# Attention values by stationary weights, carried by DMA and turned on VectorE, in a shifted-window transformer block on one core

## The chip, the cores and the metric

One Trainium2 chip, one core of it. The metric is the device time in microseconds (us) of one execution. The kernel before has a median of 2818.03 us over three runs (2814.11 to 2820.3).

## What is computed

The input x is 16 images of 192 channels, 56 x 56 pixels, float32. Layer 0 is a Swin block with 7 x 7 windows shifted by 3, six heads of 32 channels; layer 1 is a masked 3 x 3 depthwise convolution whose taps depend on the image's mean. Cut to what matters:

```python
win = shifted_windows(layernorm(x))            # (windows, 49 positions, 192 channels)
q, k, v = split(win @ qkv_w + qkv_b)           # six heads of 32 channels
attn = softmax(q @ k.T * 32**-0.5 + bias + mask)   # 49 x 49 for each window and head
out = (attn @ v) @ proj_w + proj_b             # back to the image, added to x
x1 = x + out
y = x1 + gelu(layernorm(x1) @ fc1_w + fc1_b) @ fc2_w + fc2_b
out = depthwise_conv3x3(y, taps(mean(y)))      # four of nine taps are not masked
```

The change concerns v, and how `attn @ v` reads it.

## The kernel before, in words

An image is cut into four units (`NU = 4`), each of 2 x 8 windows: channels lie in three groups (`G = 3`) of 64 partitions, and the two halves of the 128 partitions hold two rows of windows, called `ab`. So there are 64 units, and a tile such as `xs1` is 128 x 3 x 392 values, 392 being eight windows of 49 positions. All arithmetic is float32.

The kernel is one software pipeline: a Python loop over r, one round for each unit and a few rounds before and after. In a steady round r the code lists, in this order: both halves of the values of unit r with the scores of unit r between them; the scaling of the next units' inputs on POOL (`scaled2`, `scaled1`); `weighted(r-1)`, that is attention times values; the second MLP layer of unit r-3; the projection of unit r-1; queries and keys of unit r+1; the first MLP layer of unit r-2; the products of the variances (`deviations`); convolution pieces of an image that is complete; and the load of a later unit. In the rounds with r below 3, queries and keys come directly after values and scaling.

Nothing is issued in that listing. Each step is registered with `add(engine, duration, function, reads, writes)`. `Plan.order` then fixes one order for every engine: TensorE's steps stay in the order listed, and the other engines take, by assumed durations and due times, whichever ready step is most urgent. On the chip, each engine runs its fixed order and waits where an input is not there. SyncE issues nearly all DMAs in such an order too.

TensorE writes to four PSUM tiles (`ps0` to `ps3`, two banks each). `bank()` hands them out in rotation, so every product waits until the reader of the product four places earlier has emptied its tile.

Names and lines that matter:

- `values` (L656) multiplies with the windows stationary: for each window the 64 columns of `xs1` from its first position are loaded as weights, 15 of them not the window's own, and `wqkv` (192 columns) moves through. Positions therefore come out on partitions, as `weighted` needs them. `keep` (L668, ScalarE) copies each half into `v`, of which there are two buffers.
- `scores` (L551) multiplies queries (`q128`, `q2`) by keys (`kbd`, `kbd2`) in three groups; then VectorE adds the bias (L577), takes maxima (L587) and sums (L604), POOL subtracts and scales (L592, L610), and ScalarE takes the exponential (L599).
- `turn_shares` (L621) transposes the shares in 32 x 32 blocks on VectorE into `tt`, and ten DMAs (L627) carry them to `pt`, keys on partitions.
- `weighted` (L692) multiplies `v`, stationary, by `pt`; ScalarE (L719) and VectorE (L721) copy the result.
- `second_layer` (L839) ends in L826 on VectorE, `projection` (L762, L748) in L790, `first_layer` (L801) in the GELU of L813 on ScalarE. `queries_keys` is L471; VectorE writes `kbd` from it in L495.
- `deviations` (L320): ScalarE squares (L334), VectorE subtracts (L341), ScalarE takes logarithm and exponential (L350, L357), a DMA goes out (L367) and two come back (L376) into `rb`, which `scaled1` (L427, L438) and `scaled2` (L456) read. L385 is its form for the first units.
- `conv` runs on VectorE in L1114; `taps` has its product at L921.

Of the kernel before, what the change touches and what calls it, by code (L numbers as in the profile page):

```python
# [14 lines left out]
G = 3  # L15
# [3 lines left out]
NWIN = IMG // WS  # L19
N = WS * WS  # L20
UT = NWIN * N
UP = UT + 16
PW = 64 + N
NU = 4
LR = NU * WS
# [20 lines left out]
class Plan:  # L46
# [7 lines left out]
    def add(self, eng, dur, fn, reads=(), writes=(), lag=0.0, slack=60.0, by=None):  # L54
        i = len(self.ops)
        deps = set()
        reads, writes = flat(reads), flat(writes)
        for k in reads:
            if k in self.writer:
                deps.add(self.writer[k])  # L60
        for k in writes:
            if k in self.writer:
                deps.add(self.writer[k])
            deps.update(self.readers.get(k, ()))
        for k in reads:
            self.readers.setdefault(k, []).append(i)
        for k in writes:
            self.writer[k] = i
            self.readers[k] = []
        deps.discard(i)  # L70
        self.ops.append((eng, dur, fn, sorted(deps), lag, slack, by))
# [70 lines left out]
def tile_swin_then_dynamic_conv(  # L142
# [37 lines left out]
    def sb(name, *shape):  # L180
        return const.tile(list(shape), F32, tag=name, name=name)
# [20 lines left out]
    hid = sb("hid", 128, NFC, 2, UT)  # L202
    fold = sb("fold", 128, 2, 2, UT)
    sq = sb("sq", 128, G, UT)
    xs1 = sb("xs1", 128, G, UP)
    xs2 = sb("xs2", 128, G, UT)
    rb = sb("rb", 128, 2, UT)
    q128 = sb("q128", 128, 2, NWIN, 2, TL)
# [3 lines left out]
    e_t = [sb(f"e{i}", 128, 16 * N + TL) for i in range(3)]  # L212
    tt = sb("tt", 128, 2, 48, TL)
    pt = sb("pt", 128, 2, 48, TL)
    v = [sb(f"v{i}", 128, 2, 4, DIM) for i in range(2)]
    o1 = sb("o1", 128, 2, NWIN, N)
    o2 = sb("o2", 128, 2, NWIN // 2, N)
    bt1 = sb("bt1", 128, 2, 2, 4, 2, N)
# [40 lines left out]
    def P(j):  # L259
        return slice(64 * j, 64 * j + 64)  # L260
# [185 lines left out]
    def XS1(s):  # L446
        return [("xs1", g) for g in range(G)] + [
            ("xs1", "w", 0),
            ("xs1", "w", WS - SHIFT),
        ]  # L450
# [163 lines left out]
    def turn_shares():  # L614
        for j in range(3):
            for kb in range(2):
                def turn(kb=kb, j=j):

                    src = e_t[j][:, kb * TL : kb * TL + 16 * N]
                    src = src.rearrange("p (k t) -> p k t", t=N)[:, :, 0:TL]  # L620
                    nc.vector.transpose(tt[:, kb, 16 * j : 16 * j + 16], src)  # L621
                add("DVE", 0.7, turn, [("e", j), "epad"], [("t", j, kb)])
        def send(name, kb, to, of, qb):
            add(
                "SP",
                0.65,
                lambda: nc.sync.dma_start(pt[to, qb], tt[of, kb]),  # L627
                [("t", j, kb) for j in range(3)] + ["ptz"],
                [("pt", name, kb, qb)],
                lag=7.0,  # L630
            )


        for kb, n in ((0, TL), (1, 16)):
            for w in range(2):
                for qb in range(2):
                    to, of = 64 * w + TL * kb, 64 * w + TL * qb
                    send(w, kb, slice(to, to + n), slice(of, of + n), qb)
        for qb in range(2):
            send(2, 1, slice(N - 1, 128, 64), slice(TL * qb + 16, 128, 64), qb)  # L640

    def PTK():
        return [("pt", i, kb, qb) for kb in range(2) for i in range(2 + kb) for qb in range(2)]

    def values(s, parts):
        d = xs1
        for t in parts:
            p, pk = bank()

            def product(t=t, p=p):  # L650
                for i in range(2):
                    w0 = 4 * t + 2 * i
                    for g in range(G):
                        for w in (w0, w0 + 1):
                            for ab in range(2):
                                nc.tensor.matmul(  # L656
                                    p[P(w % 2), ab, i * DIM : (i + 1) * DIM],
                                    d[P(ab), g, w * N : w * N + 64],
                                    wqkv[P(ab), g, 2 * DIM :],
                                    start=(g == 0),  # L660
                                    stop=(g == G - 1),
                                    tile_position=(64 * ab, 64 * (w % 2)),
                                )

            add("PE", 1.95, product, XS1(s) + ["wqkv", "xpad"], [pk])

            def keep(t=t, p=p):
                nc.scalar.copy(  # L668
                    v[s % 2][:, :, 2 * t : 2 * t + 2, :].rearrange("p a w c -> p a (w c)"),
                    p[:, :, 0 : 2 * DIM],  # L670
                )

            add("ACT", 0.87, keep, [pk], [("v", s % 2, t)])

    def weighted(s):


        banks = [bank() for _ in range(3)]

        def product(j):  # L680
            p = banks[j][0]
            for t in range(4):
                for h in range(2):
                    for w in range(2):
                        if j < 2:
                            ab, pair, lane = j, t, 64 * h
                            slot, head = 16 * j + h * 8 + pair * 2, 2 * h
                        else:
                            ab, pair, lane = t // 2, 2 * h + t % 2, 64 * h
                            slot, head = 32 + ab * 8 + pair * 2, 4  # L690
                        shares = pt[P(w), :, slot : slot + 2, 0:QL]
                        nc.tensor.matmul(  # L692
                            p[lane : lane + 64, w, t * 128 : t * 128 + 4 * QL],
                            v[s % 2][P(w), ab, pair, head * HD : (head + 2) * HD],
                            shares.rearrange("p q k c -> p k q c"),
                            start=True,
                            stop=True,
                            tile_position=(64 * w, lane),
                        )

        for j in range(3):
            p, k = banks[j]
            add(
                "PE",
                0.7,
                lambda j=j: product(j),
                PTK() + [("v", s % 2, t) for t in range(2)] + ["ptz"],
                [k],
            )
            for i in range(4):  # L710
                lanes = slice(TL * i, TL * i + TL)
                at = (i % 2) * 2 * QL
                src = p[lanes].rearrange("p w (t c) -> p w t c", c=128)[:, :, :, at : at + N]
                if j < 2:
                    dst = o1[lanes, j].rearrange("p (t w) c -> p w t c", w=2)
                else:
                    dst = o2[lanes].rearrange("p a (t w) c -> p w (a t) c", w=2)
                if j != 1:
                    add("ACT", 0.5, lambda dst=dst, src=src: nc.scalar.copy(dst, src), [k], [("o", j, i)])  # L719
                else:  # L720
                    add("DVE", 0.56, lambda dst=dst, src=src: nc.vector.tensor_copy(dst, src), [k], [("o", j, i)])  # L721
# [466 lines left out]
    def masks():  # L1188
        def go():
            nc.vector.memset(mask2, 0.0)  # L1190
            for i in range(4):
                nc.vector.memset(mask2[i * TL : (i + 1) * TL, i % 2 : i % 2 + 1], 1.0)
        add("DVE", 0.5, go, [], ["mask2"])
        def go():
            nc.gpsimd.memset(q128, 0.0)
            nc.gpsimd.memset(q2, 0.0)
        add("POOL", 1.5, go, [], ["qpad"])
        def go():
            nc.gpsimd.memset(xs1[:, :, UT:UP], 0.0)
        add("POOL", 0.3, go, [], ["xpad"])  # L1200
        def go():
            for t in e_t:
                nc.gpsimd.memset(t[:, 16 * N :], 0.0)
        add("POOL", 0.3, go, [], ["epad"])
        def go():
            nc.gpsimd.memset(pt, 0.0)
        add("POOL", 3.0, go, [], ["ptz"])
        add("POOL", 0.2, lambda: nc.gpsimd.memset(zero, 0.0), [], ["zero"])
# [334 lines left out]
    for r in range(-2, S + 3):  # L1543
# [22 lines left out]
        early = r < 3  # L1566
        norms = [n for n, s in ((0, r + 2), (1, r - 1)) if has(s) and not early]
        if has(r):
            values(r, (0,))
            scores(r)  # L1570
            values(r, (1,))
        if 2 <= r <= 3:
            deviations([1])
        if has(r - 2):
# [12 lines left out]
            fold_proj()  # L1587
        if has(r):
            turn_shares()
        if r == S + 2:  # L1590
            ahead = early_mean(B - 1)
            next(ahead)
            second_layer(S - 1, (0,))
            for _ in ahead:
                pass
            second_layer(S - 1, (1,), lambda: taps(B - 1))
            halos(B - 1, slice(0, 2))
            second_layer(S - 1, (2,))
            halos(B - 1, slice(2, 3))
        elif has(r - 3):  # L1600
            second_layer(r - 3)
# [116 lines left out]
```

## Time and profile before

| quantity | value |
|---|---|
| median of three runs | 2818.03 us |
| the profiled execution | 2820.74 us, span 2818.9 us |
| TensorE busy | 2769.0 us (98% of the span) |
| VectorE busy | 1839.4 us (65%) |
| ScalarE busy | 1674.8 us (59%) |
| GpSimd (POOL) busy | 1582.4 us (56%) |
| moved by DMA | 189.35 MB, mean 67 GB/s |
| mean granted clock of TensorE | 0.993 |

The span runs from the first to the last instruction. Busy times are sums over the whole execution. Lines are given as L656, which is line 656 of the kernel. A steady round takes a little over 42 us. The chain of waits follows the work that ended last back through what released it; its shares are shares of the span.

### The profile page before, as it was taken

How to read it: one execution, taken by the hardware profiler on the slowest of the kernel's cores; microseconds unless marked ns; L12 is line 12 of the kernel's file. 1: busy time of each engine (PE TensorE's matmuls, PEld its weight loads, DVE VectorE, ACT ScalarE, POOL GpSimd, SP SyncE). 2: the span in 40 equal slices, each digit the busy share in tenths (PEclk: the TensorE clock that was granted, in tenths of full speed). 3: DMA queues.
4: the chain of work that ended last, by engine and by line, in shares of the span. 5: the costliest groups of instructions: out<-in, count | busy, mean ns of one | idle time of the engine just before them, and what ended most of it. 6: DMA issues, size and time to landing. Idle time of an engine off the chain costs nothing.

```text
span 2818.9 us, 79781 instructions
## 1 busy us (share of the span) xinstructions
PE 2769.0 (98%) x34405; PEld 1729.2 (61%) x34405; DVE 1839.4 (65%) x3324; ACT 1674.8 (59%) x2532; POOL 1582.4 (56%) x1436
## 2 busy tenths in 40 slices
PE   7899999999999999999999999999999999999998
PEld 5566666666566566566566666566666666665654
DVE  5555776657676675766757666675766757667673
ACT  3656556556566565666656566575565665566553
POOL 5554564565555565664655655655655655646532
PEclk9899999999999999999999999999999999999999
DMA  6412232233313233142233313233142232322131
GB/s 128 82 28 48 59 88 55 63 67 79 78 43 91 44 74 83 44 99 57 51 81 74 84 44 77 54 79 79 43 105 49 56 85 58 83 60 54 42 72 42
DMA packets 122264, 189.35 MB, mean 67 GB/s; under 512 B 31240, under 2 KB 96696, under 8 KB 121912
## 3 DMA queue, kind: packets, MB, share of 16 engines
q1 hardware_dynamic: 117144, 183.43, 29.3%
q8 instruction: 270, 4.42, 0.7%
q10 hardware_dynamic: 4768, 0.82, 0.2%
q14 instruction: 82, 0.67, 0.1%
HBM read 66.81 MB, written 38.98 MB: 38 GB/s over the span
## 4 chain that ended last, share of the span: by engine, by line
PE 95%; DVE 2%; issue 1%; ACT 1%; SPq 0%; DMA 0%; POOL 0%; ACTq 0%; DVEq 0%; POOLq 0%
PE ps L839 27%; PE ps L801 27%; PE ps L471 13%; PE ps L656 9%; PE ps L692 5%; PE ps L762 5%; PE ps L551 5%; PE ps L748 2%; PE ps L320 2%; DVE trow L934 0%; DVE hid L1114 0%; POOL xs L427 0%; DVE x L790 0%; DVE sq L935 0%; PE ps L921 0%
## 5 line engine op out<-in xcount | busy, mean ns | idle before, releaser
L839 PE MATMUL ps<-hid,wf 128*64 128x392 f32 x4608 | 774.1, 494 | 2.5 <-ACT o L719 2.5
L801 PE MATMUL ps<-xs,wf 64*128 64x392 f32 x4608 | 769.5, 489 | 0.0
L801 PEld LDWEIGHTS ps<-xs,wf 64*128 64x128 f32 x4608 | 445.9, 187 | 312.6 <-issue 0.9
L839 PEld LDWEIGHTS ps<-hid,wf 128*64 128x64 f32 x4608 | 330.3, 137 | 409.7 <-issue 370.2
L304 POOL TENSOR_TENSOR fold<-sq 128x392 f32<-128x392 f32 x128 | 131.8, 1029 | 700.5 <-PE ps L320 693.9
L813 ACT ACTIVATE hid<-ps,b1f 128x784 f32<-128x784 f32 x384 | 343.2, 914 | 145.4 <-PE ps L801 142.9
L592 POOL TENSOR_TENSOR e<-e,top 128x784 f32<-128x784 f32 x192 | 285.9, 1504 | 242.0 <-DVE top L587 242.0
L471 PE MATMUL ps<-xs,wqkv 64*128 64x392 f32 x2304 | 406.6, 502 | 11.3 <-POOL xs L438 9.7
L1114 DVE SCALAR_TENSOR_TENSOR y<-x,wt,y 128x770 f32<-128x770 f32 x270 | 305.2, 1145 | 86.1 <-ACT y L977 63.5
L471 PEld LDWEIGHTS ps<-xs,wqkv 64*128 64x128 f32 x2304 | 219.5, 189 | 177.3 <-issue 20.7
L610 POOL TENSOR_TENSOR e<-e,tot 128x784 f32<-128x784 f32 x192 | 293.2, 1537 | 55.4 <-DVE tot L605 53.3
L656 PE MATMUL ps<-wqkv,xs 64*64 64x192 f32 x6144 | 279.6, 325 | 2.1 <-issue 1.8
L456 POOL TENSOR_TENSOR xs<-x,rb 128x392 f32<-128x392 f32 x192 | 247.6, 1318 | 25.3 <-DMA rb<-rsd 25.3
L577 DVE TENSOR_TENSOR e<-ps,bt 128x784 f32<-128x784 f32 x192 | 175.2, 968 | 130.2 <-PE ps L551 130.2
L719 ACT COPY o<-ps 32x392 f32<-32x392 f32 x512 | 246.9, 482 | 9.7 <-PE ps L692 3.5
L621 DVE STREAM_TRANSPOSE tt<-e 128x512 f32<-128x512 f32 x384 | 246.3, 686 | 5.8 <-POOL e L610 4.3
L656 PEld LDWEIGHTS ps<-wqkv,xs 64*64 64x64 f32 x6144 | 225.2, 133 | 37.6 <-issue 24.5
L484 ACT ACTIVATE q<-ps,qbs 128x400 f32<-128x400 f32 (+1 forms) x128 | 68.6, 589 | 287.3 <-PE ps L471 287.3
L604 DVE TENSOR_REDUCE tot<-e 128x16 f32<-128x784 f32 x192 | 182.1, 949 | 64.8 <-ACT e L599 64.7
L341 DVE TENSOR_TENSOR m<-ps,m 128x196 f32<-128x196 f32 (+1 forms) x64 | 23.2, 362 | 304.4 <-ACT m L334 304.3
L668 ACT COPY v<-ps 128x768 f32<-128x768 f32 x128 | 102.4, 800 | 198.2 <-PE ps L656 198.2
L730 ACT ACTIVATE x<-x,pbt 128x392 f32<-128x392 f32 x192 | 105.5, 613 | 189.7 <-POOL xs L438 189.7
(126 smaller groups left out, 3594.0 us busy)
## 6 DMA issues: line engine op xcount, KB each, us to landing
pt<-tt SPq DMA_DIRECT2D x256, 192.0 KB
x<-in_x_dram SPq DMA_DIRECT2D x112, 294.0 KB
out_dram<-y SPq DMA_DIRECT2D x135, 196.0 KB
pt<-tt SPq DMA_DIRECT2D x256, 96.0 KB
rb<-rsd SPq DMA_DIRECT2D x118, 196.0 KB
out_dram<-y SPq DMA_DIRECT2D x45, 154.0 KB
x<-in_x_dram SPq DMA_DIRECT2D x16, 168.0 KB
pt<-tt SPq DMA_DIRECT2D x128, 12.0 KB
```

The lines of the kernel that those rows point to most:

```text
L456: nc.gpsimd.tensor_tensor(xs2[:, g], xv[:, g], rb[:, 1], ALU.mult)
L471: nc.tensor.matmul(p[:, ab, 0:UT], lhs_qk(ab, g, i), d[P(ab), g, 0:UT], start=(g == 0), stop=(g == G - 1), tile_position=(64 * ab, 0),)
L592: nc.gpsimd.tensor_tensor(ev, ev, top[j].broadcast_to([128, 16, N]), ALU.subtract)
L604: nc.vector.tensor_reduce(tot[j], ev, AX.X, ALU.add)
L610: nc.gpsimd.tensor_tensor(ev, ev, tot[j].broadcast_to([128, 16, N]), ALU.mult)
L621: nc.vector.transpose(tt[:, kb, 16 * j : 16 * j + 16], src)
L656: nc.tensor.matmul(p[P(w % 2), ab, i * DIM : (i + 1) * DIM], d[P(ab), g, w * N : w * N + 64], wqkv[P(ab), g, 2 * DIM :], start=(g == 0), s ...
L719: add("ACT", 0.5, lambda dst=dst, src=src: nc.scalar.copy(dst, src), [k], [("o", j, i)])
L801: nc.tensor.matmul(p[:, ab, 0:UT], wf1[P(ab), g, f * 128 : (f + 1) * 128], xs2[P(ab), g], start=(g == 0), stop=(g == G - 1), tile_position ...
L813: nc.scalar.activation(hid[:, f], p[:, :, 0:UT], AF.Gelu, bias=b1f[:, f : f + 1])
L839: nc.tensor.matmul(p[P(ab), 0, 0:UT], wf2[:, f, g * 64 : (g + 1) * 64], hid[:, f, ab], start=(f == 0), stop=(f == NFC - 1), tile_position= ...
L1114: nc.vector.scalar_tensor_tensor(dst, s_, w[:, g, t : t + 1], dst, ALU.mult, ALU.add)
```

## The change

`values` is one function of three products instead of two halves. The weights are now stationary, 64 output channels at a time, and the windows move through them: four windows of 49 positions in one matmul. Channels therefore come out on partitions, and the result must be turned. ScalarE copies it out of PSUM in two pieces per product, the first 32 positions of each window and the last 17. Their destination, `cut`, is the memory of `kbd`, which the scores have read by then. Eight DMAs on SyncE's queue move it to the new tile `vb`, blocks of 32 keys to the partitions where they belong. `turn_values` transposes `vb` in 32 x 32 blocks on VectorE into `v`, which now has one buffer. All three products come after the scores, and the turn is listed after `turn_shares`. `weighted` reads 49 partitions instead of 64, so the padding of `xs1` and its memset go.

```diff
-    def values(s, parts):
...
-                                nc.tensor.matmul(
-                                    p[P(w % 2), ab, i * DIM : (i + 1) * DIM],
-                                    d[P(ab), g, w * N : w * N + 64],
-                                    wqkv[P(ab), g, 2 * DIM :],
...
+    def values(s):
+        cut = kbd.rearrange("p a w h t -> p (a w h t)")[:, 0 : 2 * 8 * G * TL]
+        cut = cut.rearrange("p (b w g t) -> p b w g t", b=2, g=G, t=TL)
+        ck = [("kbd", 0), ("kbd", 1)]
+        xw = xs1.rearrange("p g (w i t) -> p g w i t", i=2, t=N)
+        for m in range(G):
+            p, pk = bank()
+            def product(m=m, p=p):
+                for g in range(G):
+                    for wh in range(2):
+                        for ab in range(2):
+                            nc.tensor.matmul(
+                                p[P(wh), ab, 0 : 4 * N],
+                                wqkv[P(ab), g, 2 * DIM + 64 * m : 2 * DIM + 64 * m + 64],
+                                xw[P(ab), g, :, wh],
+                                start=(g == 0),
+                                stop=(g == G - 1),
+                                tile_position=(64 * ab, 64 * wh),
+                            )
+            add("PE", 0.99, product, XS1(s) + ["wqkv"], [pk])
+            for b, n in ((0, TL), (1, N - TL)):
+                def keep(m=m, p=p, b=b, n=n):
+                    src = p[:, :, 0 : 4 * N].rearrange("p a (w t) -> p a w t", t=N)
+                    dst = cut[:, b, :, m, 0:n].rearrange("p (a w) t -> p a w t", a=2)
+                    nc.scalar.copy(dst, src[:, :, :, TL * b : TL * b + n])
+                add("ACT", 0.45 if b == 0 else 0.36, keep, [pk], ck if m == 0 and b == 0 else [("cut", m, b)])
+        done = [("cut", m, b) for m in range(G) for b in range(2)] + ck
+        for wh in range(2):
+            for i in range(2):
+                for b in range(2):
+                    def go(wh=wh, i=i, b=b):
+                        of, to = 64 * wh + TL * i, 64 * wh + TL * b
+                        nc.sync.dma_start(
+                            vb[to : to + TL, i].rearrange(flat_),
+                            cut[of : of + TL, b].rearrange(flat_),
+                        )
+                    add("SP", 0.65, go, done, [("vb", wh, i, b)], lag=4.0)
+    def turn_values():
+        for i in range(2):
+            def turn(i=i):
+                dst = v.rearrange("p a w (g i c) -> p (a w g) i c", g=G, i=2)[:, :, i]
+                nc.vector.transpose(dst, vb[:, i].rearrange("p w g t -> p (w g) t"))
+            add("DVE", 1.05, turn, [("vb", wh, i, b) for wh in range(2) for b in range(2)], [("v", i)])
...
         if has(r):
-            values(r, (0,))
             scores(r)
-            values(r, (1,))
+            values(r)
...
             turn_shares()
+            turn_values()
```

More of the change, by code (lines that the diff above doesn't have):

```diff
@@ L21 @@
 UT = NWIN * N
-UP = UT + 16
 PW = 64 + N
@@ L204, in tile_swin_then_dynamic_conv @@
     sq = sb("sq", 128, G, UT)
-    xs1 = sb("xs1", 128, G, UP)
+    xs1 = sb("xs1", 128, G, UT)
     xs2 = sb("xs2", 128, G, UT)
@@ L214, in tile_swin_then_dynamic_conv @@
     pt = sb("pt", 128, 2, 48, TL)
-    v = [sb(f"v{i}", 128, 2, 4, DIM) for i in range(2)]
+    v = sb("v", 128, 2, 4, DIM)
+    vb = sb("vb", 128, 2, 8, G, TL)
     o1 = sb("o1", 128, 2, NWIN, N)
@@ L643, in PTK @@
         return [("pt", i, kb, qb) for kb in range(2) for i in range(2 + kb) for qb in range(2)]
-    def values(s, parts):
-        d = xs1
-        for t in parts:
-            p, pk = bank()
[L650 to L656, printed above, removed]
-                                    p[P(w % 2), ab, i * DIM : (i + 1) * DIM],
-                                    d[P(ab), g, w * N : w * N + 64],
-                                    wqkv[P(ab), g, 2 * DIM :],
[L660 to L673, printed above, removed]
@@ new lines, in values @@
+    def values(s):
[4 more added lines that the diff above has]
+        for m in range(G):
+            p, pk = bank()
+            def product(m=m, p=p):
[18 more added lines that the diff above has]
+        done = [("cut", m, b) for m in range(G) for b in range(2)] + ck
+        flat_ = "p w g t -> p (w g t)"
+        for wh in range(2):
[8 more added lines that the diff above has]
+                    add("SP", 0.65, go, done, [("vb", wh, i, b)], lag=4.0)
@@ L690, in product @@
                             slot, head = 32 + ab * 8 + pair * 2, 4
-                        shares = pt[P(w), :, slot : slot + 2, 0:QL]
+                        shares = pt[64 * w : 64 * w + N, :, slot : slot + 2, 0:QL]
                         nc.tensor.matmul(
                             p[lane : lane + 64, w, t * 128 : t * 128 + 4 * QL],
-                            v[s % 2][P(w), ab, pair, head * HD : (head + 2) * HD],
+                            v[64 * w : 64 * w + N, ab, pair, head * HD : (head + 2) * HD],
                             shares.rearrange("p q k c -> p k q c"),
@@ L706, in weighted @@
                 lambda j=j: product(j),
-                PTK() + [("v", s % 2, t) for t in range(2)] + ["ptz"],
+                PTK() + [("v", i) for i in range(2)] + ["ptz"],
                 [k],
@@ L1198, in go @@
         def go():
-            nc.gpsimd.memset(xs1[:, :, UT:UP], 0.0)
-        add("POOL", 0.3, go, [], ["xpad"])
-        def go():
             for t in e_t:
```

## The prediction

> **What bounds the kernel now.** I read the page first: busy times, then the chain that ended last.
>
> ```profile
> PE 2769.0 (98%) x34405; PEld 1729.2 (61%) x34405; DVE 1839.4 (65%) x3324; ACT 1674.8 (59%) x2532; POOL 1582.4 (56%) x1436
> ...
> PE 95%; DVE 2%; issue 1%; ACT 1%; SPq 0%; DMA 0%; POOL 0%; ACTq 0%; DVEq 0%; POOLq 0%
> ```
>
> TensorE is 98% busy and 95% of the chain, with values (L656) at 9% of the span. Every other engine idles a third of the time or more, so TensorE time removed is worth its full length until another engine arrives too late. The chain through one steady round says where it stands:
>
> ```profile
> 1160.63 0.80 PE ps L320 x16
> 1161.43 2.11 PE ps L656 x48
> 1163.54 2.08 PE ps L551 x96
> 1165.62 1.95 PE ps L656 x48
> 1167.57 2.26 PE ps L692 x96
> 1169.83 12.00 PE ps L839 x72
> 1181.83 1.99 PE ps L762 x24
> 1183.82 1.16 PE ps L748 x24
> 1184.98 6.12 PE ps L471 x36
> 1191.10 11.85 PE ps L801 x72
> ```
>
> Each line begins where the one before ends: no wait at all. I call the end of L320, 1161.43, time zero of a round. What must be on time for it are the shares, the scaled inputs and emptied PSUM tiles. The timelines of SyncE and VectorE, and the stretch of DMA in which the shares travel, give the slack:
>
> ```profile
> 1161.89 0.36 DVE L341 TENSOR_TENSOR m<-ps,m 128x196 f32<-128x196 f32 x1 [0.84 <-ACT m L334]
> 1164.28 2.74 DVE L577 TENSOR_TENSOR e<-ps,bt 128x784 f32<-128x784 f32 x3 [2.03 <-PE ps L551]
> ...
> 1194.81 6.61 SPq L627 DMA_DIRECT2D pt<-tt  x10
> ...
> 1197.00:1201.50 4.50, 4.50 (x32) 2.60 (x30) 1.20 (x2) 3.86 (x6) 0.00 (x0) 1.00 1.05 213
> ```
>
> VectorE was idle before L341 (0.84 us) and before the biases (2.03 us). The ten share DMAs were all issued at 1201.4 and read by L692 from 1209.7: 8.3 us of slack, landing included. The last line's final columns are DMA share and GB/s: the engines kept up with the issue, at 213 GB/s.
>
> **What the Trainium skill says.** "TensorEngine Tiling (Array Packing)", section 64×64 Mode, gives four tiles that work side by side; both forms use all four. The trace agrees: L551's 96 instructions of 98 columns take 2.02 to 2.08 us, 0.86 ns per column over four tiles. Its section PSUM Bottleneck warns that emptying PSUM may become the limit; here the four-tile rotation decides, worked out below. "DMA: Bandwidth & Descriptors", section Anatomy of one DMA, gives about 2 us of fixed cost; I use it as an estimate for landing. It was measured on another issuing path, and no row here shows a landing. "VectorE: DVE Perf Modes", section The three transpose paths, says that VectorE turns 32 x 32 blocks only; that is why eight DMAs are needed.
>
> **The change, part by part.**
>
> 1. *Products.* Before: 96 instructions a unit (each matmul is recorded as two) of 192 columns, 2.11 + 1.95 = 4.06 us on the chain. The first half's extra 0.16 is a change of tile shape after L320; L748 shows the same, with 1.16 us for 24 instructions of 196 columns where 24 x 196 / 4 x 0.84 ns (L801: 11.85 us over 72 x 392 / 2 columns) is 0.99. After: 72 instructions of 196 columns, three times L748's 24 without its entry cost: 2.97 us. The entry cost stays, now paid by the scores. So 3.90 - 2.97 = 0.93 us a unit, times 64 = **59.5 us off the chain**. The moving operand is read in runs of 49 instead of 192; L692 reads in runs of 25 and takes 2.06 us in undelayed rounds against 2.02 by columns, so I cost runs at nothing. Bounds: gain of 0.85 to 1.10 us a unit.
>
> 2. *A new PSUM neighbour.* In the order of the changed program the scores come first after L320, and the first values product takes the tile that L320 filled. L341 on VectorE empties it, and the order puts L341 behind the first bias. That bias starts 0.74 us after the scores (1164.28 - 1163.54), takes 0.91, then L341 0.36: it ends at +2.05 to +2.1, against 2.02 to 2.08 for the scores. A wait of 0 to 0.1 us; I take 0.05 in 60 rounds, **3 us back**. Behind this wait stands everything on TensorE. Later tiles are free in time: biases end near +4 (second and third values product need the first two, from +3.1), and `weighted` starts at +5.
>
> 3. *ScalarE.* Two copies of 0.80 us (L668) become six, of 256 and 136 values per partition. From 0.80 us for 768 and 0.48 for 392 (L719): about 0.15 + 0.85 ns each, so 0.37 and 0.27, 1.9 us a unit, 0.3 more. They end near +6; the second copy ended at +7 before, so the copies and exponentials behind them are not later. Hidden.
>
> 4. *Eight DMAs.* SyncE issues one in about 0.65 us (6.61 / 10): 5.2 us, with the two of L376 in the middle of them, so from about +6 to +12.5. That makes the scaled inputs' `rb` later by up to 2 us. POOL began scaling at 1176.07 (+14.6) and finished 5.3 us before L471; with `rb` issued near +10 it still begins on time. 98 KB each is 0.79 MB, under 4 us at 213 GB/s, shorter than their issue; landing by about +14.5. Stores and loads that follow on the queue are not waited for. Hidden; bounds 0 and the second rival.
>
> 5. *VectorE.* Two turns of 768 values: 0.67 us for 512 (L621) gives 1.0 each, 2 us a unit, 129 us in all on an engine with 35% idle. The order puts them after the first two share turns, around +17, and before L826 of the third second-layer product (ends at 2.05 + 2.97 + 2.2 + 12.0 = +19.2). Queued behind is L826, with the projection's adds and, each fourth round, the mean and `taps`, whose product is due at +21.2. Turns ending at +19.3 leave all on time. The last share turns wait for POOL and L471, not for this. `weighted` comes 1.1 us earlier in the round, so its 8.3 us of slack becomes 6 to 7. Hidden.
>
> 6. *`kbd` as carrier.* Steady rounds overwrite it at +26, long after landing. In rounds 0 to 2 L471 follows directly. In round 1 the changed order puts `kbd`'s copies behind a sum and three share turns, and the second `weighted` product uses their tile: I estimate 5 us there from the durations of those rows, and 2 us more because these rounds wait for POOL anyway and cannot pocket their gain. **7 us back**, bounds 2 and 15. The dropped memset was hidden by the start.
>
> Sum: -59.5 + 3 + 7 = -49.5. The profiled execution, 2820.7, becomes 2771; it stands 2.7 above the median, so on the median **2768.5 us**.
>
> **Rivals.**
>
> *A (slower): the turn waits for its DMAs and holds VectorE.* In order, everything behind the turn waits with it. A turn that starts by +18.3 delays nothing; beyond that, sixteen rounds with `taps` lose one for one, beyond about +20.5 the others too. Gain is gone when landing is at about +21 (16 x 2.7 + 48 x 0.5 = 67), nearly 9 us after the last issue. At +22.5 it costs 16 x 4.2 + 48 x 2 = 163 us, less 52: about 2930. For it: 0.79 MB more on queues that reach a full share, and loads that sit ahead in some rounds. Against: share DMAs, larger, were used within 8.3 us of issue without one wait. Likelier is a small excess.
>
> *B: shares late.* If landing takes 5 us and VectorE or SyncE slips 2, `weighted` waits about 0.5 us in 48 rounds: 24 us, 2792.
>
> *C: the first values product waits longer.* If VectorE still convolves at time zero, L341 slips. It was idle from -0.4 in the tightest round; a slip of 0.4 us in every round gives 2790.
>
> *D: reading moving data in short runs costs TensorE its gain.* At 1.1 ns a column instead of 0.84 values take 3.9 us: no change in products, and the returns of parts 2 and 6 make 2828. L692 speaks against it. The changed order itself shows three products of twelve matmuls of 196 columns, so the work does shrink.
>
> **How the numbers follow.** The forecast has 0.74; B and C together 0.14 (both faster); A 0.08; D and mixtures of it 0.04, half of it within 0.2%. About 0.2% (5.6 us) is what a measurement of this kernel can tell from no change. So faster 0.88, same 0.03, slower 0.09. The range runs from a gain of 1.10 us a unit with little returned (2818 - 70 + 4 = 2752) to B or C (2796).
>
> **What would show it.** In the chain of the changed kernel, L320, scores, values at 2.97 to 3.1 us, `weighted`, without breaks; rounds of 41.2 to 41.4 us; VectorE's busy time up by 130 us, ScalarE's by 20; TensorE still at 98%. Wrong if waits for the turn appear before L826, or for shares before `weighted`, or if values takes over 3.3 us.

## The result, and the profile after

| kernel | median | lowest to highest | runs |
|---|---|---|---|
| before | 2819.16 us | 2814.11 to 2823.88 | 4 |
| after | 2782.45 us | 2779.58 to 2786.97 | 4 |

The ratio is 0.9872, with an interval of 0.9848 to 0.9895: 36.7 us faster, where the forecast was 49.5. The profiled execution took 2785.06 us, with a span of 2783.3. In the changed kernel values is L660, its copies L674, the eight DMAs L683, the turn L693, `weighted` L713 with its copies in L740 and L742, the second layer L860 (ending in L847), the projection L783 and L769 (ending in L811), the first layer L822. The lines named below L640 have the same numbers in both.

The busy times of the page after, and its shares of the chain by engine (PE is TensorE at its matmuls and PEld at loading weights, DVE is VectorE, ACT ScalarE, SP SyncE; a q marks an engine's queue of instructions):

```profile
PE 2731.4 (98%) x32869; PEld 1676.8 (60%) x32869; DVE 1954.0 (70%) x3452; ACT 1686.7 (61%) x2788; POOL 1552.6 (56%) x1435
...
PE 94%; DVE 3%; issue 1%; POOL 1%; ACT 1%; DMA 0%; DVEq 0%; ACTq 0%; POOLq 0%
```

TensorE gave up 37.6 us and remains the bound at 98%. VectorE rose by 114.6 us, of which the 128 turns are 119.7 at 935 ns each, and none of those is on TensorE's path. VectorE's share of the chain went from 2% to 3%. The chain of waits through one steady round shows what is (start, length, what):

```profile
1153.88 0.80 PE ps L320 x16
1154.68 0.88 PE ps L551 x32
1155.56 0.03 issue
1155.59 0.02 DVEq L577
1155.61 0.04 issue
1155.65 0.97 DVE e L577
1156.63 0.28 DVE m L341
1156.91 0.04 issue
1156.95 3.26 PE ps L660 x72
1160.21 2.06 PE ps L713 x96
1162.27 12.00 PE ps L860 x72
```

In the round of the kernel before that the prediction shows, every line of the chain was TensorE's. Here the chain leaves TensorE after the first third of the scores, runs over the first bias and L341, and comes back with the first values product. That is the PSUM neighbour of the prediction's second part, and it waits longer than forecast. VectorE's timeline of the same round shows the order (in brackets: idle before, and what ended it):

```profile
1155.65 0.97 DVE L577 TENSOR_TENSOR e<-ps,bt 128x784 f32<-128x784 f32 x1 [1.37 <-PE ps L551]
1156.55 0.35 DVE L341 TENSOR_TENSOR m<-ps,m 128x196 f32<-128x196 f32 x1
1156.81 1.84 DVE L577 TENSOR_TENSOR e<-ps,bt 128x784 f32<-128x784 f32 x2
...
1172.15 1.79 DVE L693 STREAM_TRANSPOSE v<-vb 128x768 f32<-128x768 f32 x2
```

Before 1155.65 VectorE had been idle for 1.37 us, although L341's tile was full at 1154.68 and ScalarE's square (L334) done at 1155.10; the fixed order makes it take the bias first. How often this holds TensorE up is told by the view of L341, in its list of who waited for it (us in total, times):

```profile
  PEld ps L660: 15.8, 60
```

Sixty waits of 0.26 us, one in each steady round. Below, a typical round is one that no further pause lengthens, timed from one `weighted` to the next. It went from 42.06 us to 41.50, a gain of 0.56 where 0.88 was forecast. It is not the average one: before, only 16 of 59 rounds are so short, and the median round is 42.56 us, after 41.57. The whole stretch from the fourth `weighted` to the last but one went from 2510.5 us to 2462.6 over 59 rounds, 0.81 a round, since the changed kernel also loses less in irregular pauses.

The start gives some of it back. The fourth `weighted` comes at 200.33 us, 11.9 later than before (188.41). TensorE's timeline there, and the windows around it (columns after the length: PE, PEld, DVE, ACT and POOL busy, granted clock, DMA share, GB/s):

```profile
89.45 0.92 PE L713 MATMUL ps<-pt,v 49*64 49x100 f32 x32
97.19 2.94 PE L713 MATMUL ps<-pt,v 49*64 49x100 f32 x64 [6.83 <-DVE kbd L495]
```

```profile
88.00:92.00 4.00, 2.37 (x37) 1.33 (x36) 2.42 (x4) 2.90 (x6) 3.67 (x4) 1.00 0.76 188
92.00:96.00 4.00, 0.00 (x0) 0.00 (x0) 3.97 (x7) 3.91 (x9) 1.26 (x1) 0.85 1.08 232
96.00:100.00 4.00, 2.81 (x64) 2.64 (x64) 3.46 (x6) 0.22 (x1) 0.24 (x1) 0.50 0.28 61
100.00:104.00 4.00, 4.00 (x30) 3.71 (x28) 2.34 (x5) 1.96 (x5) 0.00 (x0) 0.50 0.69 160
```

The second product of the first `weighted` waits 6.83 us for `kbd`'s copy (forecast: about 5), and after the pause TensorE runs at half clock until about 108 us. That half clock is not the wait's alone: the kernel before has it in the products behind its own first `weighted`, which waits 2.08 us for `q`:

```profile
86.45 0.92 PE L692 MATMUL ps<-pt,v 64*64 64x100 f32 x32 [2.08 <-ACT q L508]
```

```profile
88.00:92.00 4.00, 4.00 (x28) 3.43 (x30) 3.92 (x8) 3.87 (x8) 0.06 (x1) 0.56 0.02 4
92.00:96.00 4.00, 4.00 (x44) 2.73 (x44) 0.78 (x2) 3.70 (x8) 0.00 (x0) 0.59 0.63 151
```

"TensorE: Matmul & The Clock Gate" of the Trainium skill, section "What's actually happening", gives half clock after an idle stretch of about 3.4 us and full clock after about as long a busy one. In the changed kernel the first half fits: the mean clock of 0.85 between 92 and 96 us puts the fall at about 94.8, in a pause that began at 90.37. In the kernel before it does not: by the two means above the clock is halved from about 88.5 to 95.3 us, and between 80 us, when it was full, and its fall the longest pause is the 2.08 us. The recovery took longer than the page's stretch in both: TensorE stayed at half clock through some 11 us of nearly unbroken work in the one and 6.8 us in the other. Here the traces decide.

Of the 11.9 us, 6.7 lie ahead of the first `weighted` (89.45 us against 82.76) and 5.2 behind its start; part 6 below comes back to this.

### The profile page after: what moved, and what is told of

It reads as the page before. It is cut to its first block, busy times and chain, and to the rows that moved or that the text cites. A ratio compares the mean times of both kernels' runs of the same rounds, so it can differ in the third digit from the quotient of the medians.

```text
span 2783.3 us, 78087 instructions
## 1 busy us (share of the span) xinstructions
PE 2731.4 (98%) x32869; PEld 1676.8 (60%) x32869; DVE 1954.0 (70%) x3452; ACT 1686.7 (61%) x2788; POOL 1552.6 (56%) x1435
## 3 DMA queue, kind: packets, MB, share of 16 engines
q1 hardware_dynamic: 141720, 233.80, 37.6%
## 4 chain that ended last, share of the span: by engine, by line
PE 94%; DVE 3%; issue 1%; POOL 1%; ACT 1%; DMA 0%; DVEq 0%; ACTq 0%; POOLq 0%
PE ps L860 28%; PE ps L822 27%; PE ps L471 14%; PE ps L660 7%; PE ps L713 5%; PE ps L783 5%; PE ps L769 3%; PE ps L551 2%; PE ps L320 2%; DVE e L577 1%; DVE m L341 1%; POOL xs L427 0%; DVE hid L1135 0%; PE ps L1294 0%; PE ps L942 0%
## 5 line engine op out<-in xcount | busy, mean ns | idle before, releaser
L860 PE MATMUL ps<-hid,wf 128*64 128x392 f32 x4608 | 773.8, 494 | 0.0
L822 PE MATMUL ps<-xs,wf 64*128 64x392 f32 x4608 | 769.5, 489 | 0.0
L822 PEld LDWEIGHTS ps<-xs,wf 64*128 64x128 f32 x4608 | 445.9, 187 | 312.6 <-issue 0.9
L860 PEld LDWEIGHTS ps<-hid,wf 128*64 128x64 f32 x4608 | 332.0, 137 | 405.4 <-issue 371.7
L610 POOL TENSOR_TENSOR e<-e,tot 128x784 f32<-128x784 f32 x192 | 323.1, 1694 | 221.3 <-DVE tot L605 200.2
L471 PE MATMUL ps<-xs,wqkv 64*128 64x392 f32 x2304 | 409.7, 506 | 10.7 <-POOL xs L438 9.0
L1135 DVE SCALAR_TENSOR_TENSOR y<-x,wt,y 128x770 f32<-128x770 f32 x270 | 318.1, 1197 | 66.2 <-ACT y L998 45.3
L471 PEld LDWEIGHTS ps<-xs,wqkv 64*128 64x128 f32 x2304 | 221.4, 191 | 178.0 <-issue 22.4
L740 ACT COPY o<-ps 32x392 f32<-32x392 f32 x512 | 247.0, 482 | 19.2 <-PE ps L713 5.5
L660 PE MATMUL ps<-xs,wqkv 64*64 64x196 f32 x4608 | 211.3, 331 | 5.1 <-DVE rb L400 0.3
L456 POOL TENSOR_TENSOR xs<-x,rb 128x392 f32<-128x392 f32 x192 | 192.9, 1038 | 25.0 <-DMA rb<-rsd 25.0
L427 POOL TENSOR_TENSOR xs<-x,rb 128x343 f32<-128x343 f32 x192 | 186.9, 1003 | 33.8 <-PE ps L660 16.1
L304 POOL TENSOR_TENSOR fold<-x 128x392 f32<-128x392 f32 x128 | 132.3, 1033 | 127.1 <-DVE x L811 108.8
L660 PEld LDWEIGHTS ps<-xs,wqkv 64*64 64x64 f32 x4608 | 169.7, 132 | 35.9 <-DVE m L341 15.8
```

The costliest lines, as they stand in the source:

```text
L304: nc.gpsimd.tensor_tensor(f, src[:, 0], src[:, 1], ALU.add)
L471: nc.tensor.matmul(p[:, ab, 0:UT], lhs_qk(ab, g, i), d[P(ab), g, 0:UT], start=(g == 0), stop=(g == G - 1), tile_position=(64 * ab, 0),)
L610: nc.gpsimd.tensor_tensor(ev, ev, tot[j].broadcast_to([128, 16, N]), ALU.mult)
L660: nc.tensor.matmul(p[P(wh), ab, 0 : 4 * N], wqkv[P(ab), g, 2 * DIM + 64 * m : 2 * DIM + 64 * m + 64], xw[P(ab), g, :, wh], start=(g == 0), ...
L822: nc.tensor.matmul(p[:, ab, 0:UT], wf1[P(ab), g, f * 128 : (f + 1) * 128], xs2[P(ab), g], start=(g == 0), stop=(g == G - 1), tile_position ...
L860: nc.tensor.matmul(p[P(ab), 0, 0:UT], wf2[:, f, g * 64 : (g + 1) * 64], hid[:, f, ab], start=(f == 0), stop=(f == NFC - 1), tile_position= ...
```

## The experiments

Four questions were open: whether the order of L341 and the first bias is what costs 0.3 us a round; whether the order "scores first" causes it or the new products do; what of the start comes from `kbd` as carrier; and whether the DMAs and turns cost anything. All times are medians; ratios are to runs of the kernel before on the same chip.

### again: the changed kernel once more

> The changed kernel once more, so that the three beside it have it on the same chip. Expected as before: about 2782 us, a typical steady round of 41.5 us, with values at 3.26 us on the chain after a wait of about 0.26 us for L341.

2780.5 us, ratio 0.9865 (0.9845 to 0.9886). It repeats the result and is the measure for the runs beside it.

### skip: the first values product in another PSUM tile

```diff
             scores(r)
+            bank()
             values(r)
```

One tile of the rotation is passed over, so the first values product takes the tile that the first bias empties.

> The changed kernel with one PSUM tile of the rotation left unused between scores and values, so that the first values product takes the tile of the first scores product and not that of the variances. Neighbour theory (the missing gain of a steady round is the wait for L341 and the restart of TensorE behind it, 0.3 us a round): values stretch from 3.26 to about 3.05 us, the wait of 16 us in all before it goes, a typical round of 41.2 us, about 2764 us. Rival (the products are slower than worked out because of their shape and their reads in runs): values stays at 3.26 us, about 2782 us.

2782.79 us, ratio 0.9875 (0.9856 to 0.9893): no gain. The wait for L341 did vanish; a steady round's chain has scores at 2.18 us and values at 3.03 to 3.08. But a new wait took its place, as the view of TensorE's waits shows, and POOL's waits show where it comes from (us in total, times, longest; the first row had 9.0 us in 3 in the changed kernel, the second had none among its ten largest):

```profile
PE ps L471 <- POOL xs L438: 28.4, 22, 4.5
```

```profile
POOL xs L427 <- DMA rb<-rsd: 22.4, 22, 1.9
```

With nothing waiting for L341 any more, the planner put it behind all three biases. In a round with time zero 1485.03 it ends at +3.9 instead of +2.2, the result of L357 leaves on SyncE's queue (L367) at +9.6 instead of +3.1, behind four of the new DMAs, and the two loads of `rb` follow the other four and four stores:

```profile
1490.70 3.79 SPq L683 DMA_DIRECT2D vb<-kbd  x4
1494.59 0.62 SPq L367 DMA_DIRECT2D rsd<-rs  x1
1495.26 2.43 SPq L683 DMA_DIRECT2D vb<-kbd  x4
1497.78 2.47 SPq L1018 DMA_DIRECT2D out_dram<-y  x4
1500.35 1.34 SPq L376 DMA_DIRECT2D rb<-rsd  x2
```

`rb` is issued at +15.3 instead of +8.6, POOL's scaling begins at 1505.17, after 1.25 us of waiting for it, and L471 starts at +23.7 instead of +22.7. So, by the trace, the new stall is the late `rb` on SyncE's queue; no run tried to take it away. The chain here also has a landing on it: the Trainium skill's "DMA: Bandwidth & Descriptors", section "Anatomy of one DMA", gives about 2 us of fixed cost, measured on another issuing path, and the chain has 3.96 us between the end of an issue of `rb` and POOL, while the engines moved 200 GB/s. The measured figure includes moving the 196 KB and is about twice the page's.

### head: another carrier in the first three rounds

```diff
+        if s < 3:
+            cut = [yt[b].rearrange("p r c -> p (r c)")[:, 0:nb] for b in range(2)]
+            ck = [("y", 0), ("y", 1)]
+        else:
             (the halves of kbd, as before)
...
+            for y in yt:
+                nc.gpsimd.memset(y, 0.0)
```

`yt`, two tiles that the convolution does not use yet, carries the blocks of the first three units.

> The changed kernel with the output tiles y0 and y1, which are unused so early, as carrier of the values in rounds 0 to 2 in place of kbd. Carrier theory (the lost time of the start is kbd's copies waiting for the eight DMAs and for what was put ahead of them): the 6.8 us wait of weighted for L495 in round 1 goes, and with it some of the half clock that follows such a wait; 6 to 10 us faster than the changed kernel, about 2774 us. Rival (the start is slow because of where the low clock falls, not because of kbd): within 3 us of the changed kernel.

2775.1 us, ratio 0.9847 (0.9829 to 0.9864), 5.4 us below again, between the 6 to 10 expected and the rival's 3. With mfirst in place the same edit gives 3.4 (mhead, below). The intervals overlap both times, so the times alone do not settle it, but the mechanism is seen: the 6.83 us wait is gone, and `weighted` waits 4.0 us in two pieces for `q` (L508) instead, as in the kernel before. From the first `weighted` to the fourth the profiled execution takes 104.0 us, the changed kernel 110.9 and the kernel before 105.7.

### best: skip and head together

> Both edits together: the tile left unused between scores and values, and y0 and y1 as carrier in rounds 0 to 2. If both theories hold, their gains add: 18 and 8 us under the changed kernel, about 2756 us. If the start is a matter of where the low clock falls, about 2764 us. If the products are slow by shape, about 2774 us.

2781.33 us, ratio 0.9869 (0.9851 to 0.9886). It misses by 25 us, because it has skip's new wait, with 27.6 us in 22 times.

### mfirst: L341 ordered ahead of the first bias

```diff
-            0.4,
+            0.25,
```

This is the duration that the planner assumes for the square of L334. With 0.25 it believes that L341 is ready before the first bias; nothing else is edited. In the traces, line by line, ScalarE and POOL keep their order, VectorE's differs only by L341's place in 59 rounds, and SyncE's by the place of one DMA of the values in 33.

> The changed kernel with one number of the planner: the assumed duration of the square of the variances (L334) is 0.25 us instead of 0.4, so that VectorE's order puts L341 ahead of the first bias in the steady rounds, as in the kernel before; tiles and POOL's order stay. Neighbour theory: L341 ends at +0.82 and the first values product needs its tile at +2.2, so the wait goes as it did with a tile left unused, and this time POOL's scaled inputs stay on time: scores and values together 0.27 us shorter a round, 16 us in all, about 2765 us. Rival (the wait only moves to the next late thing, as happened with the unused tile): about 2780 us.

2765.13 us, ratio 0.9811 (0.9797 to 0.9826), as expected. VectorE's timeline has the new order, and the wait is gone:

```profile
1190.75 0.36 DVE L341 TENSOR_TENSOR m<-ps,m 128x196 f32<-128x196 f32 x1 [2.83 <-ACT m L334]
1191.20 2.74 DVE L577 TENSOR_TENSOR e<-ps,bt 128x784 f32<-128x784 f32 x3
```

A typical round is 41.20 us instead of 41.50, within the prediction's 41.2 to 41.4: 0.30 times 60 is 18 us, and the ratios differ by 0.0054 to 0.0061, 15 to 17 us. The order on VectorE is the cause of nearly all of the shortfall in the steady rounds.

### mhead: mfirst and head together

> The same, and y0 and y1 as carrier in rounds 0 to 2. Expected by the sum of both: 16 and 5 us under the changed kernel, about 2759 us. If L341's place only moves the wait, as the carrier alone: about 2775 us.

2761.69 us, ratio 0.9798 (0.9782 to 0.9815). A second time, on another chip and beside the two runs below, called mhead2:

> The best version so far once more (L341 ahead of the first bias, y0 and y1 as carrier in rounds 0 to 2), as base for the two beside it: 2762 us.

2754.6 us, ratio 0.9792 (0.9776 to 0.9808), and this version beats both kernels. Its chain (values is L666 here, `weighted` L719):

```profile
1217.09 2.18 PE ps L551 x96
1219.27 3.03 PE ps L666 x72
1222.30 2.06 PE ps L719 x96
```

Scores and values are 5.21 us, where the kernel before took 2.11 + 2.08 + 1.95 by the fence of the prediction, 6.14, or 6.08 in rounds that nothing delayed. The typical round is 0.86 us shorter than before, against 0.88 in the forecast. The fourth `weighted` comes at 187.03 us, before the 188.41 of the kernel before; in mhead, which is the same kernel, it comes at 193.58. How little the weights of the first product wait is seen in the timelines of PEld, first the changed kernel, then this one:

```profile
1154.61 2.06 PEld L551 LDWEIGHTS ps<-kbd,q 64*64 64x64 f32 x96 [0.31 <-issue]
1156.95 2.90 PEld L660 LDWEIGHTS ps<-xs,wqkv 64*64 64x64 f32 x72 [0.28 <-DVE m L341]
```

```profile
1217.02 2.06 PEld L551 LDWEIGHTS ps<-kbd,q 64*64 64x64 f32 x96 [0.31 <-issue]
1219.01 2.93 PEld L666 LDWEIGHTS ps<-xs,wqkv 64*64 64x64 f32 x72
```

From the scores' first load to that of values is 2.34 us with the wait and 1.99 without.

### moved: the old products in the new order

```diff
-            values(r, (0,))
             scores(r)
-            values(r, (1,))
+            values(r, (0, 1))
```

This is the kernel before with both halves of values after the scores, and nothing else of the change.

> The kernel before, with one part of the change alone: both halves of the values come after the scores, with the windows stationary as ever and no DMA, turn or new carrier. Neighbour theory: the first half takes the tile of the variances, and VectorE's order has L341 behind the first bias, so each round gains a wait of about 0.26 us and 0.05 of restart: 0.3 us a round, 18 us slower than the kernel before, about 2836 us. Rival (the wait belongs to the new products): no difference, 2818 us.

2830.89 us, ratio 1.0038 (1.0025 to 1.0052): slower by 11 to 13 us, where 18 was expected. Its chain leaves TensorE at the same place, with the old values, L656:

```profile
1203.38 0.88 PE ps L551 x32
...
1204.35 0.97 DVE e L577
1205.33 0.28 DVE m L341
...
1205.65 4.13 PE ps L656 x96
```

Its typical round is 42.37 us, 0.31 more than before. So the price belongs to the order, and it is the same 0.3 us whichever products are made. Sixty times 0.31 is the 18 expected; the rest is that it loses less in irregular rounds than the kernel before, of which more below. (Its profiled execution, 2824.94 us, is one of the two fastest of five.)

### cont: moving data without gaps

```diff
-        xw = xs1.rearrange("p g (w i t) -> p g w i t", i=2, t=N)
+        xw = xs1.rearrange("p g (i q) -> p g i q", i=2)
...
-                                xw[P(ab), g, :, wh],
+                                xw[P(ab), g, wh],
```

The 196 columns are read as one stretch instead of four runs of 49, so the windows come out in another order than the rest of the kernel expects.

> The changed kernel with the moving operand of the values read as 196 consecutive columns (windows 0 to 3 and 4 to 7) instead of four runs of 49 (every second window), so the values belong to other windows than in the reference. If the runs cost, four instructions side by side take 166 ns as in L748 and not 168 as now, and the values stretch is 0.04 us shorter a round (3 us in all). If they do not, nothing changes. In both cases the wait for L341 stays.

A single execution took 2786.38 us, no difference that one run could show. In the profile, grouped by line and shape, TensorE's busy time for values is the finer measure (busy us, mean ns of one); the first fence is cont, the second the changed kernel:

```profile
L660 PE MATMUL ps<-xs,wqkv 64*64 64x196 f32 x4608 | 208.7, 331 | 4.7 <-DVE x L811 0.3 <-DVE m L341 0.2
```

```profile
L660 PE MATMUL ps<-xs,wqkv 64*64 64x196 f32 x4608 | 211.3, 331 | 5.1 <-DVE rb L400 0.3 <-issue 0.3 <-DVE x L811 0.3
```

2.6 us in 64 units, 0.04 a unit, by one trace of each: the short runs cost next to nothing. Rival D, with 3.9 us for values, is refuted in its size.

### dma2 and turn3: the hidden work doubled and tripled

Both are edits of mhead. dma2 issues each of the eight DMAs twice; turn3 makes each turn three times.

```diff
+                    for _ in range(2):
-                    add("SP", 0.65, go, done, [("vb", wh, i, b)], lag=4.0)
+                        add("SP", 0.65, go, done, [("vb", wh, i, b)], lag=4.0)
```

```diff
+            for _ in range(3):
-            add("DVE", 1.05, turn, ...)
+                add("DVE", 1.05, turn, ...)
```

> That version with each of the eight DMAs of the values issued twice, to the same place. The 16 issues take 10.4 us of SyncE's queue instead of 5.2 and end near +18 of a round, not +12.5; 50 MB more are moved in all. Cover theory (SyncE's queue and the landing are hidden by the second MLP layer, with several us to spare): within 5 us of 2762. Rival A (the turn waits for its DMAs and holds what VectorE must do for TensorE): every us past the spare time comes back in each of some 60 rounds, 20 us or more slower, with waits of TensorE on L811, L847 or the mean's product.

> The same version with each of the two turns of vb made three times, to the same place: four more instructions of 0.93 us, 3.7 us a round, some 240 us more on VectorE, which goes from 70% to about 79% busy. Cover theory (VectorE's added work stands beside TensorE): within 8 us of 2762. Rival (VectorE is the next bound in the rounds with convolution): 15 us or more slower, with TensorE waiting for VectorE's lines.

dma2 took 2752.28 us, ratio 0.9781 (0.9767 to 0.9796), against mhead2's 2754.6: no cost for 5.2 us more of SyncE's queue and 0.79 MB more a round. In a round with time zero 1182.27 the issues now last to +17.8 instead of +13.0. But the planner knows of the added issues: in dma2 it puts a piece of convolution ahead of the turns, which start at +21.2 instead of mhead2's +17.3, and only five of 128 waited for their DMAs, 4.8 us in all. So the run shows that there is room for later turns, not that turns at +17.3 would stand DMAs that land later:

```profile
1187.94 2.47 SPq L689 DMA_DIRECT2D vb<-kbd  x4
1190.52 1.93 SPq L376 DMA_DIRECT2D rb<-rsd  x2
1192.49 7.62 SPq L689 DMA_DIRECT2D vb<-kbd  x12
```

turn3 took 2761.09 us, ratio 0.981 (0.9796 to 0.9825), 6.5 us over mhead2, though the two intervals overlap. The busy times of its page:

```profile
PE 2710.6 (98%) x32869; PEld 1669.5 (61%) x32869; DVE 2127.5 (77%) x3708; ACT 1683.9 (61%) x2788; POOL 1518.3 (55%) x1437
```

VectorE carries 176 us more for those 6.5 us. The typical round is still 41.20 us; in the two profiled executions 2.8 us of the difference arise before the fourth `weighted` and 5.0 between there and the last but one, in rounds outside the typical ones. Here too the planner moves turns to later places. The single turns of the change are hidden.

## Why the prediction was right, and where it was off

**Part 1, the products: right.** Forecast 0.93 us a unit on the chain, less the wait. Without the wait the chain gains 0.87 (6.08 less 5.21) and a typical round 0.86. Values takes 3.03 us rather than 2.97, four side-by-side instructions 168 ns rather than 165; cont puts up to 0.04 us of that on the short runs. The entry cost of 0.16 us did move to the scores: 2.18 us instead of 2.02. The skill's "TensorEngine Tiling (Array Packing)", section "Key Properties", says that a change of tiling mode drains TensorE, which fits; what the trace shows is the 0.16 us, not the draining itself.

**Part 2, the PSUM neighbour: right mechanism, wrong size.** This is the step that failed. It said that the bias "starts 0.74 us after the scores" and that L341 ends at +2.05 to +2.1, so "a wait of 0 to 0.1 us; I take 0.05 in 60 rounds, 3 us back". Measured: the bias starts at +0.97, L341 ends at +2.22, the wait is 0.26 and the round 0.30 longer: 18 us instead of 3. The 0.74 was taken from a round in which the scores followed 64-row products. Part 1 had just given the scores the entry cost after L320, and part 2 then used the old start of their first reader; the entry cost would account for 0.16 of the 0.23. It also compared L341 with the scores' end as seen on the matmuls, while the weights of values are loaded 1.99 us after those of the scores. mfirst and moved show the cause from both sides: 15 to 17 us gained without it, 11 to 13 lost by it alone.

**Parts 3 to 5, copies, DMAs and turns: right.** The copies of L674 are 126.7 us of ScalarE instead of 102.4 (forecast: 20 more); as the two copies of a product overlap in the trace, ScalarE's busy time rose by only 11.9. SyncE issues the eight DMAs from +6.0 to +13.0 (forecast +6 to +12.5), with the two of L376 in the middle:

```profile
1160.67 2.46 SPq L683 DMA_DIRECT2D vb<-kbd  x4
1163.24 1.92 SPq L376 DMA_DIRECT2D rb<-rsd  x2
1165.21 2.52 SPq L683 DMA_DIRECT2D vb<-kbd  x4
1187.85 6.59 SPq L627 DMA_DIRECT2D pt<-tt  x10
```

The shares of the last line, all issued by 1194.4, are read by L713 from 1201.66: 7.2 us of slack, where part 5 said 6 to 7. The turns run from +17.5 to +19.3 (forecast +17 to +19.3), and in the whole execution one of them waited for its DMAs, 1.7 us. So rival A did not come, and neither did B, as `weighted` has no recurring wait for shares. VectorE gained 114.6 us instead of 130, a turn being 0.94 us and not 1.0.

**Part 6, the start: the carrier about right, the rest not foreseen.** Forecast 7 us back, beside three rounds' gain that is not pocketed, so some 3 us behind by then; measured 11.9. The carrier's part, forecast 5, came out near that: between the first and the fourth `weighted` the changed kernel takes 6.9 us more than head, and by the medians the edit is worth 5.4 and 3.4. Another 6.7 us lie ahead of the first `weighted`, where the prediction had nothing: 89.45 us against 82.76. Much of that can be chance. mhead and mhead2 are the same kernel and reach this point at 90.10 and 83.33 us, with the low clock in different places: the second L471, 36 instructions in both, takes 9.08 us in mhead and 6.20 in mhead2. What part of these 6.7 us the change causes is not settled.

**What hid the failure.** The rounds are 0.81 us shorter on average but only 0.56 in the typical one. The remaining 0.25, about 15 us over 59 rounds, was in no part of the prediction, and that the total came so near is in part luck: without it the gain would be about 22 us. It comes from irregular rounds: the kernel before has pauses that add to its typical rounds in several places, among them 9.6 us recorded as waits of L692, L839, L656 and L551; the changed kernel has 2.3. Some 2 us more are in the rounds with `taps`, every fourth, which take 0.66 us more than the typical one before and 0.52 after. For 7.1 of the 9.6 us the profile names nothing that TensorE waited for. moved, with the old products, averages 0.30 above its typical round, the changed kernel 0.24 and the kernel before 0.49, so by these three traces most of it came with the order and not with fewer instructions. Which mechanism is at work was not tried and stays open. Sum against the profiled executions: 33 us from typical rounds and 15 from irregular ones, less 11.9 at the start and 0.4 at the end, is 35.7; the spans differ by 35.6. Against the forecast of 49.5 that is 15 more lost to the wait, 4 to products that gain 0.86 us a round instead of 0.93, and 9 more at the start than reckoned, set off in part by the 15 of irregular rounds.

**Rival C** named the right symptom, values waiting for L341, but a convolution that delays VectorE as its cause. VectorE was idle at time zero in every steady round, for at least 0.39 us by then; the bias ahead of L341 was the cause. A slip in the chances changes nothing: half of D's 0.04 is 0.02, so "same" adds up to 0.02 and "slower" to 0.10.

## What to carry to other kernels

When a product is moved behind another, follow its PSUM tile to the reader that empties it, and recompute when that reader's own predecessors in its engine's order can start after the move: an entry cost that is charged to one product delays everything that reads it. In a planner's fixed order, a tie of a few tenths of a microsecond on an idle engine can decide a wait in every round; here a changed assumed duration of 0.15 us was worth 16 us. A way round a wait that frees the planner to reorder (skip) must be followed down the queues that it touches, since a late small DMA cost as much as the wait that was removed.

## What the runs showed of the hardware that was not expected

- A wait of 0.26 us in a weight load lengthened the round by 0.30 us (41.50 with it, 41.20 without). What makes the other 0.04 was not tried.
- After 6.83 us of idle, TensorE's granted clock stayed at 0.50 through about 11 us of nearly unbroken work. In the kernel before it stayed there for 6.8 us after a pause of only 2.08. Where such stretches fall at the start moved one and the same kernel by 6.5 us (fourth `weighted` at 187.03 and 193.58).
- Reading the moving operand in runs of 49 float32 values instead of one stretch of 196 cost 2.6 us in 4608 instructions, by one trace of each.
- A 32 x 32 block transpose of 128 x 768 float32 on VectorE takes 935 ns at the median, 0.27 us more than one of 128 x 512.
